# Gathered rows transposed half by DMA, half by TensorE, in the expert loop of a fused attention and mixture-of-experts kernel

## The chip, the cores and the metric

The kernel runs on one core of a Trainium2 chip. A core has five engines with instruction streams of their own: TensorE (PE; its weight loads are shown apart as PEld), VectorE (DVE), ScalarE (ACT), GpSimd (POOL) and SyncE (SP), which here does nothing but issue DMAs. Sixteen DMA engines move data between DRAM and the on-chip memory SBUF; matmuls write to the accumulator memory PSUM. Each engine takes its instructions strictly in order and waits on semaphores.

The metric is the device time in microseconds (us) of one execution, the median of several runs. The kernel before took 1259.69 us (three runs, 1258.86 to 1262.91).

## The reference, cut to what matters

The input is x with 8 sequences of 512 tokens, 512 numbers each, all in 32-bit floats.

```python
xn = layernorm(x)
s = attention(xn)            # 16 heads of 32, linear attention with decay, gate, group norm, Wo
g = silu(ffn(xn))
out = x + s * g

def ffn(xn):                 # over all 4096 tokens
    probs = softmax(xn @ gate_w.T)               # 16 experts
    weights, chosen = top_k(probs, 4); weights /= weights.sum()
    mixed = sum over e of comb[:, e] * ((silu(xn @ Wg[e]) * (xn @ Wu[e])) @ Wd[e])
    shared = (silu(xn @ sWg) * (xn @ sWu)) @ sWd
    return mixed + shared * sigmoid(xn @ shared_gate_w)
```

Each expert is a 512 to 128 to 512 network. Only the four chosen experts of a token count, so the kernel computes only these.

## The kernel before, in words

**Stage one, about 0 to 320 us: routing, and attention of the first two sequences.** Sequences pass through `norm` (statistics on DVE, a power on POOL, centring on DVE; the normalised rows go to the DRAM table `xn_d`), `turn` (transposes on PE, copies on ACT), `route_1`, `route_2` (expert choice) and `share_1`, `share_2` (the shared expert; its result goes to DRAM as `sh_d`). The generator `first` (L882) hands out these pieces, and they are issued between the matmuls of attention for sequence 0. At most three sequences' x are in SBUF at a time (tag `x`, three buffers); `load_x(b + 3)` is issued at the beginning of step b of `first`. `sort` and `table` then put every (token, expert) pair into blocks of 128 rows that belong to one expert: at most 143 blocks (NB). `slot` lists, for each block, which rows of `xn_d` it takes. A row of `xn_d` has 512 floats and 16 expert weights.

**Stage two, about 320 to 795 us: the block loop.** For each block i:

- `gather(i)` (L958): POOL issues an indirect DMA that brings the block's 128 rows from `xn_d` into a buffer `xg` (five of these).
- `transpose_x(i)` (L965): PE loads the offset of the block's expert into a register and transposes the four 128x128 parts of the rows into PSUM; ACT copies the result to `xt` in SBUF.
- `gate_up(i)` (L980): four matmuls of 256 columns (each shown as two records); Silu on ACT and a product on DVE give `slb`.
- `transpose_h(i)` (L993): PE transposes `slb`, DVE copies it to `hT`.
- `down(i)` (L1000): a matmul of 512 columns (two records); DVE scales by the token's expert weight, which stands in the row `xg`, and SP stores `y` to DRAM.

The loop's body (L1023 to L1035) orders these as gate_up(i), transpose_x(i + 2), gather(i + 3), down(i - 1), transpose_h(i). A scheduler then fixes the order on each engine; on PE it is gate_up(i), transpose_x(i + 2), down(i - 1), transpose_h(i). The expert weights of all 16 experts (`wexp`) stay in SBUF during the loop.

**Stage three, about 795 to 1275 us.** Attention of sequences 2 to 7, while `mixture` gathers each token's four rows of `y` and adds them up on POOL and DVE; the output is x + s * silu(...).

Of the kernel before, what the change touches and what calls it, by code (L numbers as in the profile page):

```python
# [10 lines left out]
F32 = mybir.dt.float32  # L11
F16 = mybir.dt.float16
I32 = mybir.dt.int32
U32 = mybir.dt.uint32
AF = mybir.ActivationFunctionType
ALU = mybir.AluOpType
AX = mybir.AxisListType

P = 128
# [4 lines left out]
NC = N // C  # L24
# [69 lines left out]
def tile_block(ctx: ExitStack, tc: tile.TileContext, a: dict, out: bass.AP):  # L94
# [9 lines left out]
        return pp.tile([P, 512], F32, tag=tag, name=name, bufs={"a": 4, "k": 1, "m": 1, "d": 2}[tag])  # L104


    xn_d = dram.tile([B * N, D + E], F32, name="xn_d", tag="xn_d")
    xT_d = [dram.tile([P, KC * N], F32, name=f"xT_d{b}", tag=f"xT_d{b}") for b in range(B)]
    sh_d = [dram.tile([N, D], F32, name=f"sh_d{b}", tag=f"sh_d{b}") for b in range(B)]
    s_d = [dram.tile([N, D], F32, name=f"s_d{b}", tag=f"s_d{b}") for b in range(FIRST)]  # L110
# [112 lines left out]
    def norm(b):  # L223
        xs = xs_of[b]
        mv = p1.tile([P, NC, 2], F32, tag="mv", name=f"mv_{b}", bufs=2)
        rstd = p1.tile([P, NC], F32, tag="rstd", name=f"rstd_{b}", bufs=2)
        tiles = [slice(t, t + 1) for t in range(NC)] if b == 0 else [slice(0, NC)]

        def stand(engine):
            return behind(engine) if b < 2 else nullcontext()  # L230

        def center(ts):
            for t in range(ts.start, ts.stop):
                with stand(DVE):
                    nc.vector.tensor_scalar(
                        xs[:, t, :], xs[:, t, :], mv[:, t, 0:1], rstd[:, t : t + 1],
                        ALU.subtract, ALU.mult)

        for i, ts in enumerate(tiles):
            for t in range(ts.start, ts.stop):  # L240
                st = p1.tile([P, 6], F32, tag="st", name=f"st_{b}_{t}", bufs=4)
                with stand(DVE):
                    nc.vector.bn_stats(st, xs[:, t, :])
                with stand(DVE):
                    nc.vector.bn_aggr(mv[:, t, :], st)
            with stand(POOL):
                nc.gpsimd.tensor_scalar(rstd[:, ts], mv[:, ts, 1], LN_EPS, None, ALU.add)
            with stand(POOL):
                nc.gpsimd.tensor_tensor(
                    rstd[:, ts], rstd[:, ts],  # L250
                    root.to_broadcast([P, ts.stop - ts.start]), ALU.pow)
            if i:
                center(tiles[i - 1])
        center(tiles[-1])
        nc.sync.dma_start(
            xn_d[b * N : (b + 1) * N, :D].rearrange("(t p) d -> p t d", p=P), xs)

    def turn(b):

        xs = xs_of.pop(b)  # L260
        if b:
            xT = p1.tile([P, KC, N], F32, tag="xT1", name=f"xT1_{b}", bufs=2)
        else:
# [81 lines left out]
    def share_2(b):  # L345
        h, sg = h1_of.pop(b), sg_of.pop(b)
        xT1_of.pop(b)
        sh = p1.tile([P, NC, D], F32, tag="sh1", name=f"sh1_{b}", bufs=2)
        for t in range(NC):
            py = bank("dmaa"[t], f"pys_{b}_{t}")  # L350
            with on_pe():
                nc.tensor.matmul(
                    py, lhsT=h[:, t * P : (t + 1) * P], rhs=sw[:, KC * 2 * F :],
                    start=True, stop=True)
            if t % 2:
                nc.vector.tensor_scalar(sh[:, t, :], py, sg[:, t : t + 1], None, ALU.mult)  # L356
            else:
                nc.scalar.activation(sh[:, t, :], py, AF.Copy, scale=sg[:, t : t + 1])
        nc.sync.dma_start(sh_d[b].rearrange("(t p) d -> p t d", p=P), sh)


    def sort():
# [3 lines left out]
        for r in range(TOPK):  # L366
# [2 lines left out]
                w4[:, :, r : r + 1].to_broadcast([P, NT, E]), ALU.mult)  # L369
            if r:  # L370
                nc.gpsimd.tensor_tensor(wt, wt, wr, ALU.add)
        nc.sync.dma_start(xn_d[:, D:].rearrange("(t p) e -> p t e", p=P), wt)
        mf = mask.rearrange("p e t -> p (e t)")
        total = p1.tile([P, E * NT], F32, tag="lT", name="total", bufs=1)
        at = p1.tile([P, E, NT], F32, tag="at", name="at")
# [506 lines left out]
    def first():  # L882

        for b in range(B):
            if b + 3 < B:
                load_x(b + 3)
            route_1(b)
            yield
            share_1(b)
            yield  # L890
            if b + 2 < B:
                norm(b + 2)
            if b + 1 < B:
                turn(b + 1)
                yield
            route_2(b)
            yield
            share_2(b)
            yield
        next(sorting)  # L900
# [48 lines left out]
    for e in range(E - LATE, E):  # L949
        nc.sync.dma_start(wexp[:, e, :], a["experts"][:, e, :])  # L950
    left.close()


    blkp = left.enter_context(
        tc.tile_pool(name="blkp", bufs=1, side="left", reuse_waits="tile"))
    xg_of, xt_of, off_of, h_of, hT_of, done, gone = {}, {}, {}, {}, {}, [], []

    def gather(i):  # L958
        xg = blkp.tile([P, D + E], F32, tag="xg", name=f"xg_{i}", bufs=5)
        nc.gpsimd.indirect_dma_start(  # L960
            out=xg, out_offset=None, in_=xn_d,
            in_offset=bass.IndirectOffsetOnAxis(ap=slot[:, i : i + 1], axis=0))
        xg_of[i] = xg

    def transpose_x(i):  # L965
        with tc.issue_after(done[-1]) if done else nullcontext():
            _, (off_of[i],) = nc.values_load_multi_w_load_instructions(
                of_block(0, i), engines=[mybir.EngineType.PE], min_val=0,
                max_val=(E - 1) * WE, bass_reorder=False,
                skip_runtime_bounds_check_because="sort() takes the minimum with the last place")  # L970
        xg = xg_of[i]
        pt = bank("a", f"pt_{i}")
        for k in range(KC):
            nc.tensor.transpose(  # L974
                pt[:, k * P : (k + 1) * P], xg[:, k * P : (k + 1) * P], ident)
        xt = att.tile([P, KC, P], F32, tag="qT" if i % 2 else "kT", name=f"xt_{i}", bufs=2)
        nc.scalar.copy(xt.rearrange("p k t -> p (k t)"), pt)  # L977
        xt_of[i] = xt

    def gate_up(i):  # L980
        off = off_of[i]
        xt = xt_of.pop(i)
        pg = bank("k" if i % 2 else "m", f"pgu_{i}")
        for k in range(KC):
            nc.tensor.matmul(  # L985
                pg[:, : 2 * F], lhsT=xt[:, k, :], rhs=wflat[:, bass.ds(off + k * 2 * F, 2 * F)],
                start=(k == 0), stop=(k == KC - 1))
        sl = blkp.tile([P, F], F32, tag="sl", name=f"slb_{i}")
        nc.scalar.activation(sl, pg[:, :F], AF.Silu)  # L989
        nc.vector.tensor_tensor(sl, sl, pg[:, F : 2 * F], ALU.mult)  # L990
        h_of[i] = sl

    def transpose_h(i):  # L993
        ph = bank("a", f"ph_{i}")
        done.append(nc.tensor.transpose(ph[:, :P], h_of.pop(i), ident).ins)
        hT = blkp.tile([F, P], F32, tag="hT", name=f"hT_{i}")
        nc.vector.tensor_copy(hT, ph[:, :P])  # L997
        hT_of[i] = hT

    def down(i):  # L1000
        py = bank("d", f"py_{i}")
        nc.tensor.matmul(  # L1002
            py, lhsT=hT_of.pop(i), rhs=wflat[:, bass.ds(off_of.pop(i) + KC * 2 * F, D)],
            start=True, stop=True)
        with tc.issue_after(gone[-1]) if gone else nullcontext():
# [3 lines left out]
                skip_runtime_bounds_check_because="sort() takes the minimum with the last place")  # L1009
        y = att.tile([P, D], F32, tag="tmp", name=f"y_{i}", bufs=TMP)  # L1010
        gone.append(nc.vector.tensor_scalar(  # L1011
            y, py, xg_of.pop(i)[:, bass.ds(at, 1)], None, ALU.mult).ins)
        nc.sync.dma_start(y_d[i * P : (i + 1) * P, :], y)


    for i in range(3):
        gather(i)
    for t in range(NC):
        spill(FIRST - 1, t, project(FIRST - 1, t))
        if t in (1, 2):  # L1020
            transpose_x(t - 1)
    on_of.pop(FIRST - 1)
    for i in range(NB + 1):  # L1023
        if i < NB:
            gate_up(i)
        if i == 2:
            gate_3(FIRST)
        if i + 2 < NB:
            transpose_x(i + 2)
        if i + 3 < NB:  # L1030
            gather(i + 3)
        if i:
            down(i - 1)
        if i < NB:
            transpose_h(i)  # L1035
    left.close()
    right.close()

# [150 lines left out]
```

## Time and profile before

| | before |
|---|---|
| median of the runs | 1259.69 us |
| the profiled execution | 1276.38 us |
| its span, first to last instruction | 1274.6 us |
| mean granted TensorE clock | 0.992 |
| block loop: first gate/up matmul to last down product | 335 to 795 us |
| gathers in the loop (POOL, xg from xn_d) | 143, mean 947 ns of issue |
| stores of y (SP) | 143, 256 KB each |
| DMA traffic | 201 MB, mean 158 GB/s |

How to read it: the page shows one execution, with the profiler on. It was 16.7 us longer than the runs' median. A group's "idle before" is the time in which that engine did nothing just ahead of these instructions, and the name after the arrow is what ended it. An engine that is idle but is not the last to be ready costs nothing. A matmul's record is longer than the spacing of matmuls, because they overlap; spacing is read from start to start.

### The profile page before, as it was taken

The page shows a single profiled execution, that of the slowest core. Times are in us where ns is not written, and L with a number is a line of the kernel's source. Part 1 is how long each engine was busy: PE and PEld are TensorE (multiplying, and loading weights), DVE is VectorE, ACT ScalarE, POOL GpSimd, SP SyncE. Part 2 cuts the span into 40 slices and gives each one's busy share as a digit, 9 for nine tenths or more (in the row PEclk, how much of TensorE's full clock was granted, in tenths as well). Part 3 has the DMA queues.
Part 4 walks back from the last instruction along what each step waited for, and adds up shares of the span by engine and source line. Part 5 has one row for each costly group of instructions (what it writes and reads, how often), then busy time and mean ns, then how long its engine had stood idle before and what let it go on. Part 6 is the DMA issues. An engine that isn't in the chain of part 4 may idle for free. (4 is left out here: it accounts for less than half of the span.)

```text
span 1274.6 us, 21687 instructions
## 1 busy us (share of the span) xinstructions
PE 1218.6 (96%) x8085; PEld 724.0 (57%) x8085; DVE 763.7 (60%) x1668; ACT 343.0 (27%) x623; POOL 423.5 (33%) x398
## 2 busy tenths in 40 slices
PE   7999999989999999999999999999999999989997
PEld 3445544455577777777777776454544544445453
DVE  6377646996233333333333333777969779498784
ACT  3334433121322222222222222114141131311420
POOL 2000003000233222222332321660885857758311
PEclk9999999999999999999999999999999999999999
DMA  9775221450555555555555554840754636435111
GB/s 324 272 278 198 91 109 42 160 204 25 185 168 172 173 168 168 169 166 162 169 174 161 168 168 137 311 141 1 241 172 136 222 98 214 135 121 162 42 33 68
DMA packets 84934, 201.02 MB, mean 158 GB/s; under 512 B 15008, under 2 KB 15776, under 8 KB 82912
## 3 DMA queue, kind: packets, MB, share of 16 engines
q1 hardware_dynamic: 63152, 127.41, 27.5%
q0 software_dynamic: 21680, 72.23, 19.4%
q8 instruction: 67, 1.10, 0.3%
q14 instruction: 35, 0.29, 0.1%
HBM read 127.25 MB, written 72.35 MB: 157 GB/s over the span
## 5 line engine op out<-in xcount | busy, mean ns | idle before, releaser
L960 POOL DMA_INDIRECT xg<-xn_d,slot x143 | 135.4, 947 | 435.1 <-DVE hT L997 323.2
L985 PE MATMUL pgu<-wexp,xt 128*128 x1144 | 270.8, 379 | 0.0
L985 PEld LDWEIGHTS pgu<-wexp,xt 128*128 128x128 f32 x1144 | 206.2, 190 | 63.2 <-ACT xt L977 38.4
L1011 DVE TENSOR_SCALAR y<-py,xg 128x512 f32<-128x512 f32 x143 | 107.4, 751 | 111.4 <-PE py L1002 111.4
L1058 POOL DMA_INDIRECT yg<-y_d,posi x128 | 138.8, 1084 | 47.4 <-DMA m<-sh_d 20.0
L990 DVE TENSOR_TENSOR slb<-slb,pgu 128x128 f32<-128x128 f32 x143 | 41.1, 288 | 185.0 <-ACT slb L989 185.0
L1002 PE MATMUL py<-wexp,hT 128*128 x286 | 146.4, 594 | 0.0
L538 PE MATMUL pv<-wv,xT 128*128 128x512 f32 x256 | 121.0, 611 | 2.9 <-DVE sh L356 1.6
L580 PE MATMUL pk<-xT,wk 128*128 128x512 f32 x256 | 122.2, 618 | 0.0
L989 ACT ACTIVATE slb<-pgu 128x128 f32<-128x128 f32 x143 | 39.6, 277 | 289.1 <-PE pgu L985 289.0
L580 PE MATMUL pq<-xT,wq 128*128 128x512 f32 x256 | 115.9, 593 | 0.0
L709 PE MATMUL pw<-wo,on 128*128 128x512 f32 x224 | 102.6, 603 | 4.9 <-DVE m L1086 4.9
L1093 POOL TENSOR_TENSOR xo<-xo,m 128x512 f32<-128x512 f32 x30 | 44.7, 1492 | 168.2 <-DVE m L1086 162.5
L977 ACT COPY xt<-pt 128x512 f32<-128x512 f32 x143 | 83.8, 586 | 39.1 <-PE pt L974 39.1
L974 PE MATMUL pt<-ident,xg 128*128 128x128 f32 x572 | 86.5, 274 | 5.8 <-DMA xg<-xn_d,slot 4.2
L974 PEld LDWEIGHTS pt<-ident,xg 128*128 128x128 f32 x572 | 69.4, 141 | 27.4 <-PE pgu L985 10.1
L650 DVE TENSOR_TENSOR sc<-ps,dmask 128x512 f32<-128x512 f32 x128 | 79.4, 682 | 1.4 <-PE ps L634 1.4
L538 PEld LDWEIGHTS pv<-wv,xT 128*128 128x128 f32 x256 | 46.4, 193 | 59.5 <-issue 54.0
L580 PEld LDWEIGHTS pq<-xT,wq 128*128 128x128 f32 x256 | 47.3, 191 | 52.2 <-issue 51.4
L580 PEld LDWEIGHTS pk<-xT,wk 128*128 128x128 f32 x256 | 47.0, 194 | 49.0 <-issue 46.7
L709 PEld LDWEIGHTS pw<-wo,on 128*128 128x128 f32 x224 | 41.8, 193 | 55.0 <-issue 46.5
L585 ACT ACTIVATE sk<-pk 128x512 f32<-128x512 f32 x32 | 19.0, 595 | 128.5 <-PE pk L580 110.1
(160 smaller groups left out, 1577.3 us busy)
## 6 DMA issues: line engine op xcount, KB each, us to landing
y_d<-y SPq DMA_DIRECT2D x143, 256.0 KB
wexp<-in_experts SPq DMA_DIRECT2D x16, 768.0 KB
xn_d<-x SPq DMA_DIRECT2D x8, 1024.0 KB
sh_d<-sh SPq DMA_DIRECT2D x8, 1024.0 KB
m<-sh_d SPq DMA_DIRECT2D x32, 256.0 KB
xo<-in_x SPq DMA_DIRECT2D x32, 256.0 KB
out<-xo SPq DMA_DIRECT2D x32, 256.0 KB
x<-in_x SPq DMA_DIRECT2D x7, 1024.0 KB
```

Of the source, the lines that this page charges most:

```text
L538: nc.tensor.matmul(pv, lhsT=xT_of[b][:, k, t * P : (t + 1) * P], rhs=wv[:, k, :], start=(k == 0), stop=(k == KC - 1))
L580: nc.tensor.matmul(ps, lhsT=w[:, k, g * P : (g + 1) * P], rhs=xT_of[b][:, k, :], start=(k == 0), stop=(k == KC - 1))
L650: nc.vector.tensor_tensor(s, pss[j].rearrange("p (c t) -> p c t", t=C), dmask[:, g * HG + j].unsqueeze(1).to_broadcast([P, NC, C]), ALU.mult)
L709: nc.tensor.matmul(pw, lhsT=on_of[b][:, g, t * P : (t + 1) * P], rhs=wo[:, g, :], start=(g == 0), stop=(g == G - 1))
L960: nc.gpsimd.indirect_dma_start(out=xg, out_offset=None, in_=xn_d, in_offset=bass.IndirectOffsetOnAxis(ap=slot[:, i : i + 1], axis=0))
L974: nc.tensor.transpose(pt[:, k * P : (k + 1) * P], xg[:, k * P : (k + 1) * P], ident)
L977: nc.scalar.copy(xt.rearrange("p k t -> p (k t)"), pt)
L985: nc.tensor.matmul(pg[:, : 2 * F], lhsT=xt[:, k, :], rhs=wflat[:, bass.ds(off + k * 2 * F, 2 * F)], start=(k == 0), stop=(k == KC - 1))
L1002: nc.tensor.matmul(py, lhsT=hT_of.pop(i), rhs=wflat[:, bass.ds(off_of.pop(i) + KC * 2 * F, D)], start=True, stop=True)
L1011: gone.append(nc.vector.tensor_scalar(y, py, xg_of.pop(i)[:, bass.ds(at, 1)], None, ALU.mult).ins)
L1058: nc.gpsimd.indirect_dma_start(out=yg, out_offset=None, in_=y_d, in_offset=bass.IndirectOffsetOnAxis(ap=posi[:, r, g : g + 1], axis=0))
L1093: nc.gpsimd.tensor_tensor(xo, xo, m, ALU.add)
```

## The change

What it does, part by part:

- **The table.** `xn_d` is now declared as 16-bit integers, with the same bytes per row. The first 256 floats of a row are stored as before. The last 256 floats are stored as two runs of 256 16-bit values: all lower halves, then all upper halves. The new function `halves(b)` makes them: for each of a sequence's four tiles, a POOL copy sorts the halves into `hs` (four buffers) and SP stores `hs`. It stands in `first` after `norm(b + 2)`; `load_x(b + 3)` moves from the head of the step to behind it.
- **Memory.** `share_2` uses six buffers of one tile each, not two of four tiles, and stores each tile by itself: four DMAs of 256 KB in place of one of 1 MB. For the loop there are seven row buffers (`homes`), three of them in one of the buffers of `v`; the row buffers are fixed tiles used in turn.
- **The transpose.** For block i SP issues one DMA transpose (`turn_rows`) of the 512 16-bit values of the second half, 128 rows, into one of four places in `pls`. PE transposes only the first two of the four parts. `join(i)` on ACT copies these two from PSUM, and writes the transposed lower and upper halves in turn into the other half of `xt`, so that each pair is a float again. `xt` has two buffers where it had four.
- **The stagger.** The body is now turn_rows(i + 2), join(i + 1), gate_up(i), transpose_x(i + 2), transpose_h(i - 1), down(i - 2), gather(i + 4), and runs for one step more. `sl` and `hT` get two buffers. The register load of the expert's offset moves from `transpose_x` to the head of `gate_up`.

```diff
-    xn_d = dram.tile([B * N, D + E], F32, name="xn_d", tag="xn_d")
+    xn_d = dram.tile([B * N, 2 * (D + E)], U16, name="xn_d", tag="xn_d")
...
         nc.sync.dma_start(
-            xn_d[b * N : (b + 1) * N, :D].rearrange("(t p) d -> p t d", p=P), xs)
+            xn_d[b * N : (b + 1) * N, :D].rearrange("(t p) d -> p t d", p=P),
+            xs[:, :, : D // 2].bitcast(U16))
+
+    def halves(b):
+        xs = xs_of[b]
+        for t in range(NC):
+            hs = p1.tile([P, D], U16, tag="hs", name=f"hs_{b}_{t}", bufs=4)
+            with behind(POOL):
+                nc.gpsimd.tensor_copy(
+                    hs.rearrange("p (h d) -> p h d", h=2),
+                    xs[:, t, D // 2 :].bitcast(U16).rearrange("p (d h) -> p h d", h=2))
+            g = b * NC + t
+            nc.sync.dma_start(xn_d[g * P : (g + 1) * P, D : 2 * D], hs)
+        xs_of.pop(b)
...
-        sh = p1.tile([P, NC, D], F32, tag="sh1", name=f"sh1_{b}", bufs=2)
         for t in range(NC):
+            sh = p1.tile([P, D], F32, tag="sh1", name=f"sh1_{b}_{t}", bufs=6)
...
-        nc.sync.dma_start(sh_d[b].rearrange("(t p) d -> p t d", p=P), sh)
+            nc.sync.dma_start(sh_d[b][t * P : (t + 1) * P, :], sh)
...
         for b in range(B):
-            if b + 3 < B:
-                load_x(b + 3)
             route_1(b)
             yield
             share_1(b)
             yield
             if b + 2 < B:
                 norm(b + 2)
+            halves(b)
+            if b + 3 < B:
+                load_x(b + 3)
...
+    more = att.tile([P, 2 * NC * D], U16, tag="v", name="more", bufs=2)
+    homes = [blkp.tile([P, ROW], U16, tag=f"xg{j}", name=f"xg{j}") for j in range(4)]
+    homes += [more[:, j * ROW : (j + 1) * ROW] for j in range(3)]
+    pls = [att.tile([P, 2, KC, P], U16, tag="kT", name=f"pl{j}", bufs=2) for j in range(2)]
...
+    def turned(i):
+        return pls[i % 2][:, i // 2 % 2]
+
+    def turn_rows(i):
+        if i < NB:
+            nc.sync.dma_start_transpose(turned(i), row(i)[:, D : 2 * D])
+
     def transpose_x(i):
+        if i < NB:
+            pt_of[i] = bank("a", f"pt_{i}")
+            for k in range(KP):
+                nc.tensor.transpose(
+                    pt_of[i][:, k * P : (k + 1) * P],
+                    row(i).bitcast(F32)[:, k * P : (k + 1) * P], ident)
+
+    def join(i):
+        if i < NB:
+            xt = att.tile([P, KC, P], F32, tag="qT", name=f"xt_{i}", bufs=2)
+            nc.scalar.copy(
+                xt[:, :KP, :].rearrange("p k t -> p (k t)"), pt_of.pop(i)[:, : KP * P])
+            nc.scalar.copy(
+                xt[:, KP:, :].bitcast(U16).rearrange("p k (t h) -> p h k t", h=2),
+                turned(i).rearrange("p (h k) t -> p h k t", h=2))
+            xt_of[i] = xt
...
-    for i in range(NB + 1):
-        if i < NB:
-            gate_up(i)
+    join(0)
+    for i in range(NB + 2):
+        turn_rows(i + 2)
+        join(i + 1)
+        gate_up(i)
         if i == 2:
             gate_3(FIRST)
-        if i + 2 < NB:
-            transpose_x(i + 2)
-        if i + 3 < NB:
-            gather(i + 3)
-        if i:
-            down(i - 1)
-        if i < NB:
-            transpose_h(i)
+        transpose_x(i + 2)
+        transpose_h(i - 1)
+        down(i - 2)
+        gather(i + 4)
```

In the scheduled order of the changed kernel, SP takes the transpose of block k + 7 directly behind the store of y of block k, and the store of y of block k + 1 behind that transpose. On ACT the join of the DMA's halves stands ahead of the copy from PSUM, and both ahead of Silu of the block before.

## The prediction

> **What bounds the kernel now.** I began with the summary at the head of the page, which names the busiest engine:
>
> ```profile
> PE 1218.6 (96%) x8085; PEld 724.0 (57%) x8085; DVE 763.7 (60%) x1668; ACT 343.0 (27%) x623; POOL 423.5 (33%) x398
> ```
>
> TensorE (PE) is busy for 96% of the span, but its ends are modelled, so I went to the stage that the change is about. The windows view gives the block loop (410 to 780 us) and then two single blocks, one from the middle and one from the loop's end:
>
> ```profile
> 410.00:780.00 370.00, 365.90 (x1736) 270.33 (x1735) 142.57 (x347) 99.92 (x232) 109.60 (x116) 1.00 0.53 168
> 503.37:506.51 3.14, 3.14 (x17) 2.36 (x16) 1.24 (x3) 0.87 (x3) 0.94 (x1) 1.00 0.52 170
> 788.76:791.53 2.77, 2.77 (x13) 1.91 (x11) 1.23 (x3) 0.28 (x1) 0.00 (x0) 1.00 0.28 104
> ```
>
> The columns are length, then PE, PE weight loads, VectorE (DVE), ScalarE (ACT), GpSimd (POOL), clock, DMA share, GB/s. 116 blocks in 370 us are 3.19 us each; an undisturbed one takes 3.14 us. The third row is a block with nothing left to transpose (13 matmuls, not 17): 2.77 us. Four transposes are therefore worth 0.36 us or a little more. The timeline, PE alone, splits a block by start times:
>
> ```profile
> 503.37 1.02 PE L1002 MATMUL py<-wexp,hT 128*128 x2
> 504.24 0.27 PE L995 MATMUL ph<-ident,slb 128*128 128x128 f32 x1
> 504.34 1.89 PE L985 MATMUL pgu<-wexp,xt 128*128 x8
> 506.07 0.60 PE L974 MATMUL pt<-ident,xg 128*128 128x128 f32 x4
> 506.51 1.02 PE L1002 MATMUL py<-wexp,hT 128*128 x2
> ```
>
> From start to start: down 0.87, transpose of h 0.10, gate/up 1.73, four transposes of x 0.44 (0.43 in the block before). Nothing is idle between them, so in this stage PE alone sets the time, and a transpose costs 0.107 us, not the 0.274 us of its record. Everything else has room: per block ACT 0.87, DVE 1.24, POOL 0.94 us, and the DMA engines 0.53 x 3.19 = 1.7 us. The groups say how often PE waited there:
>
> ```profile
> L974 PE MATMUL pt<-ident,xg 128*128 128x128 f32 x464 | 70.1, 274 | 4.1 <-DMA xg<-xn_d,slot 3.8
> L977 ACT COPY xt<-pt 128x512 f32<-128x512 f32 x116 | 67.9, 585 | 33.4 <-PE pt L974 33.4
> L989 ACT ACTIVATE slb<-pgu 128x128 f32<-128x128 f32 x116 | 32.1, 277 | 237.7 <-PE pgu L985 237.7
> ```
>
> 3.8 us in 370 are late gathers. One is visible: POOL issued a gather at 495.63 and its transpose began only at 499.77, after an idle 0.23; so 4.1 us from issue to use, while another with 3.84 us (492.40 to 496.24) made it.
>
> [...] the multiplication by cos (L589) takes 676 ns in 100:200, where POOL does nothing, and 1032 and 1180 ns (qT, kT) in 1000:1100, where POOL adds tiles.
>
> **Part 1, two of four transposes leave PE.** 143 x 2 x 0.107 = 30.7 us, as long as PE stays the bound at 3.14 - 0.21 = 2.92 us a block.
>
> **Part 2, the DMA transpose (143, 128 KB each, on SP's queue).** Unknown, so bounded. [...] A gain below nothing is excluded: the queues had no such work. I estimate [...] with issue, start and completion like a gather's, 3 us from issue to landing. Three tests then:
> - *DMA engines*: [...] They become the bound above 1.2 us per transpose, and the gain is gone at about 1.4.
> - *SP*: a store of y issues in 0.33 us (timeline). In the order after, SP alternates: transpose of block k+7, store of y of block k+1. It waits at the transpose for the gather, and that store stands behind it; y has four buffers, so a microsecond there hurts nobody. SP needs 0.33 + the transpose's issue, under 2.92 unless issue alone exceeds 2.5 us.
> - *The loop through the buffers*: seven row buffers, so gather k+7 waits for y of k. From there: y 0.75, to POOL 0.27, gather 4.0 to landing, transpose T, join 1.0, handover 0.1; then three block periods from gate/up to y. Seven periods in all, hence 4 periods = 6.1 + T. At 2.92 us a period T may be 5.5 us, at 3.14 us 6.4. My 3 us leaves 2.5.
>
> **Part 3, the joining on ACT.** The copy from PSUM halves: between 277 ns (128 wide) and 585 ns (512), so 0.38. The join is 512 elements: 0.6, at worst 1.2 if its two-byte strided writes run at half rate. With Silu 1.3 to 1.9 of 2.92: hidden. The join waits for the DMA and Silu of the block before queues behind it; Silu's result is wanted one block later than before (the deeper stagger), and that is the cover. If the DMA is more than about 2.5 us late, gate/up itself is late next.
>
> **Part 4, the stagger.** The transposition of h and the down projection now come one and two blocks after gate/up: no PE time, one more drain step at the end, about 0.5 us. PE's register load of the expert offset moves from two blocks ahead to directly before the first gate/up matmul. What covers it is the queued down work, 0.87 us, where before it was gate/up matmuls of 0.21 each; I take 0 and keep 0.3 us a block as the bad end. Row buffers 5 to 7: the gather gets nearly 7 us from issue to the PE transpose instead of 4; half of the late gathers, 2 us, is gained. The first transposes at entry: +0.5.
>
> **Part 5, the first stage pays for the halves.** 32 POOL copies of 128x512 16-bit elements. [...] the two-input adds here take 1.28 us. [...] DVE's two-input rotations there are some 25 us of work, a fifth of the time beside POOL: about +1 us. The stores to DRAM carry the same bytes in 24 (shared expert) + 32 (halves) more issues, about 0.35 us each, which stand in SP's queue. What counts is the loads of x, now behind them:
>
> ```profile
> 63.40 1.31 SPq L145 DMA_DIRECT2D x<-in_x  x1
> 75.26 0.36 SPq L255 DMA_DIRECT2D xn_d<-x  x1
> 78.56 1.28 DVE L243 BATCH_NORM_STATS2 st<-x 128x6 f32<-128x512 f32 x2
> 80.00:90.00 10.00, 10.00 (x30) 3.99 (x29) 8.53 (x20) 1.62 (x3) 1.26 (x2) 1.00 0.74 258
> 100.00:110.00 10.00, 9.52 (x69) 4.39 (x69) 8.96 (x37) 5.94 (x8) 0.00 (x0) 1.00 0.89 319
> ```
>
> The fifth sequence's x (counting from 0) was loaded at 63.40, for statistics at 78.56. After the change SP holds that load behind the store of sequence 4, which stood at 75.26: it starts at about 77 and, at 1 MB, lands near 83. DVE, in order, stands for 4 to 5 us. It is 85 to 90% busy here, PE is the bound, so most of it is absorbed by work already in PE's queue until about 108, where PE already waits for DVE. I take 3.5 us of PE time [...] range 0 to 12.
>
> **Sum.** -30.7 - 2 + 4.5 + 1.0 (entry and drain) + 1.2 (a block in ten whose join is late by about 0.1, as with gathers today) = -26. The profiled execution took 1276.4 us (span 1274.6), so 1250 by it; the runs' median is 16.7 us lower, and nothing suggests that the difference lies in these steps: 1259.7 - 26 = **1234 us**.
>
> **Rivals.**
> - *The DMA transpose bounds the loop (ends slower).* Place: the 16 engines, or the transposes one after another. It decides from 1.4 us of engine time, or 2.8 us in series with the store's issue. At 2.0 us of engine time a block takes 3.7 us: +0.5 x 143 = +70, about 1330 us[...]. For it: two-byte elements scattered over partitions, on queues already 53% busy. [...] 24%.
> - *The wait returns through the buffers.* T between 5.5 and 6.7 us: each further us is 36 us, so 1246 to 1275. For it: gathers are already late now and then at 4 us. 10%.
> - *PE's sequencer or the first stage eats it.* A register load exposed by 0.3 us is 43 us, with the sum above 1277; or 12 us of first-stage stalls, 1242. 6%.
> - *Better than said*, below 1222, if the first stage absorbs all and the gathers' waits all go: 3%. That the change doesn't do what it says is excluded: the order shows two transposes per block on PE instead of four.
>
> The forecast keeps 57%, with a range of its own of 1222 to 1246. About 0.3% (4 us) is what a measurement of this kernel can tell. The second rival's 10% fall 4 faster, 2 within, 4 slower, the third's 6% half within and half slower. Faster: 57 + 3 + 4 = 64%; within 0.3%: 2 + 3 = 5%; slower: 24 + 4 + 3 = 31%. For 8 in 10 the range must reach into the first rival to its milder half: 1222 to 1335.
>
> **What would show it.** Right: blocks of 2.9 us in the middle of the loop; PE without idle before gate/up; ACT about 1.3 us a block; the weight loads of gate/up not waiting for the join. Wrong: gate/up waiting for ACT and ACT for the DMA of the transposed halves; a DMA share near 1; SP's transposes with long issues; in the first stage, DVE waiting at the statistics around 80 us for x, and PE idle near 108 us for DVE.

## The result, and the profile after

The changed kernel took 1250.41 us (median of seven runs, 1248.2 to 1256.08); the kernel before, beside it, 1260.88 us (seven runs). The ratio is 0.9916, with a 95% interval of 0.9895 to 0.9937: faster by 10.5 us, where 26 were forecast. The profiled execution took 1250.12 us, its span is 1248.4 us.

The head of the page after, with TensorE's granted clock in 40 slices of the span:

```profile
PE 1188.4 (95%) x7799; PEld 703.8 (56%) x7799; DVE 772.1 (62%) x1668; ACT 399.7 (32%) x766; POOL 448.9 (36%) x430
...
PEclk9979899999989999999999999999989999999999
```

PE lost 30 us of work (1218.6 before), ACT gained 57, POOL 25. The third, fifth and twelfth digit of the clock, slices around 78, 140 and 359 us, are below 9; in the page before all forty are 9:

```profile
PEclk9999999999999999999999999999999999999999
```

That is the first hint of where the gain went.

The loop did what was said. The windows view of the kernel after, the loop's middle and one block (columns as in the prediction):

```profile
400.00:760.00 360.00, 359.41 (x1599) 267.48 (x1598) 151.54 (x369) 154.30 (x369) 115.69 (x123) 1.00 0.94 227
500.80:503.71 2.91, 2.91 (x14) 2.19 (x13) 1.24 (x3) 1.27 (x3) 0.94 (x1) 1.00 0.97 188
```

123 blocks in 360 us: 2.93 us each, PE idle for 0.6 us in all. But the DMA share rose from 0.53 to 0.94. The timeline of PE for that block:

```profile
500.80 1.89 PE L1030 MATMUL pgu<-wexp,xt 128*128 x8
502.53 0.38 PE L1004 MATMUL pt<-ident,xg 128*128 128x128 f32 x2
502.74 0.27 PE L1042 MATMUL ph<-ident,slb 128*128 128x128 f32 x1
502.85 1.02 PE L1051 MATMUL py<-wexp,hT 128*128 x2
503.71 0.38 PE L1030 MATMUL pgu<-wexp,xt 128*128 x1
```

From start to start: gate/up 1.73, two transposes 0.21, transpose of h 0.11, down 0.86: 2.91 us, for the 2.92 of the prediction. The groups on ACT:

```profile
L1013 ACT COPY xt<-pl 128x512 uint16<-128x512 uint16 x143 | 109.6, 767 | 156.3 <-DMA pl<-xg 92.3 <-DMA pl<-more 63.8
L1011 ACT COPY xt<-pt 128x256 f32<-128x256 f32 x143 | 51.3, 359 | 0.0
```

The join takes 0.77 us and waits for the DMA transpose in 135 of 143 blocks, 156 us in all; PE hardly sees it, with 0.7 us of idle before gate/up in the whole loop.

The gain was lost ahead of the loop. The first gate/up matmul starts at 357.6 us, 22.6 us later than before (335.0). One place shows how; the timelines of SP, of DVE and of PE in the kernel after, in this order:

```profile
62.64 1.18 SPq L270 DMA_DIRECT2D xn_d<-hs  x2
63.92 0.40 SPq L147 DMA_DIRECT2D x<-in_x  x1
```

```profile
71.16 0.69 DVE L245 BATCH_NORM_STATS2 st<-x 128x6 f32<-128x512 f32 x1 [3.42 <-DMA x<-in_x]
71.77 0.67 DVE L572 COPY g<-pg 128x512 f32<-128x512 f32 x1
```

```profile
72.54 2.04 PE L577 MATMUL pf<-g,four 128*128 128x512 f32 x2 [4.61 <-issue]
```

The same in the kernel before:

```profile
41.25 0.58 SPq L145 DMA_DIRECT2D x<-in_x  x1
```

```profile
67.68 0.69 DVE L555 COPY g<-pg 128x512 f32<-128x512 f32 x1 [0.27 <-PE pg L551]
68.29 1.28 DVE L243 BATCH_NORM_STATS2 st<-x 128x6 f32<-128x512 f32 x2
```

```profile
68.47 1.10 PE L560 MATMUL pf<-g,four 128*128 128x512 f32 x2 [0.86 <-issue]
```

The load of x of sequence 4 leaves SP at 63.92 us (41.25 before), behind stores of the halves. Its statistics on DVE wait 3.42 us for it. Behind them on DVE stands the copy `g`, which PE needs (the matmuls of `pg` ahead of it end at 67.9 us, it begins at 71.77), and PE stands for 4.61 us. So two things came together: x is late, and the scheduled order on DVE has the statistics ahead of `g`, where before `g` stood ahead of them. Then comes what the prediction did not have at all. The windows view of the kernel after; look at the clock, third column from the end:

```profile
66.00:70.00 4.00, 1.94 (x11) 0.27 (x9) 0.69 (x1) 0.00 (x0) 0.00 (x0) 1.00 0.88 250
70.00:74.00 4.00, 1.46 (x2) 0.50 (x2) 2.54 (x5) 0.00 (x0) 0.00 (x0) 0.50 1.02 413
78.00:82.00 4.00, 3.87 (x19) 3.88 (x19) 2.79 (x4) 3.35 (x8) 2.52 (x4) 0.50 0.31 101
86.00:90.00 4.00, 4.00 (x10) 1.61 (x9) 1.43 (x7) 1.54 (x3) 0.00 (x0) 0.87 1.03 370
```

PE's last work before the gap ends at 67.9 us. From 70.0 to about 87 us the clock is at half (0.50), and the two matmuls of `pf` take 2.04 us where they took 1.10 before. The clock falls 2.1 us after the last work, and comes back 14.5 us after work begins again, 9 us after the last of two small gaps (0.78 and 0.67 us). A gap of 2.7 us before 121.5 us was followed by 10 us at 0.50, one of 2.8 us at the loop's entry by 3.4 us of it. But a gap of 3.06 us before 30.74 us in the same trace was followed by work at 1.00; what decides it is not shown. Behind the three gaps of 4.61, 2.73 and 2.83 us, work of 6.5, 4.6 and 1.7 us was lost at the lower clock (PE's busy time times what the clock lacks of 1). Where PE sets the time, these three then cost 1.6 to 2.7 times their length, an estimate from these numbers.

### The profile page after: what moved, and what is told of

The parts are those of the page before. It is cut to its first block, busy times and chain, and to the rows that moved or that the text cites. A ratio compares the mean times of both kernels' runs of the same rounds, so it can differ in the third digit from the quotient of the medians.

```text
span 1248.4 us, 21569 instructions
## 1 busy us (share of the span) xinstructions
PE 1188.4 (95%) x7799; PEld 703.8 (56%) x7799; DVE 772.1 (62%) x1668; ACT 399.7 (32%) x766; POOL 448.9 (36%) x430
## 3 DMA queue, kind: packets, MB, share of 16 engines
q8 instruction: 64, 1.05, 0.3%
## 5 line engine op out<-in xcount | busy, mean ns | idle before, releaser
L1030 PEld LDWEIGHTS pgu<-wexp,xt 128*128 128x128 f32 x1144 | 217.4, 191 | 92.6 <-issue 32.1
L989 POOL DMA_INDIRECT xg<-xn_d,slot x83 | 78.4, 945 | 287.6 <-DVE y L1060 172.0
L1013 ACT COPY xt<-pl 128x512 uint16<-128x512 uint16 x143 | 109.6, 767 | 156.3 <-DMA pl<-xg 92.3
L1107 POOL DMA_INDIRECT yg<-y_d,posi x128 | 141.9, 1108 | 49.5 <-DMA m<-sh_d 22.1
L989 POOL DMA_INDIRECT more<-xn_d,slot x60 | 56.4, 941 | 114.4 <-DVE y L1060 113.5
L1060 DVE TENSOR_SCALAR y<-py,xg 128x512 f32<-128x512 f32 x83 | 62.3, 750 | 31.4 <-PE py L1051 31.4
L1060 DVE TENSOR_SCALAR y<-py,more 128x512 f32<-128x512 f32 x60 | 45.0, 750 | 20.7 <-PE py L1051 20.6
```

The lines of the kernel that those rows point to most:

```text
L989: nc.gpsimd.indirect_dma_start(out=row(i), out_offset=None, in_=xn_d, in_offset=bass.IndirectOffsetOnAxis(ap=slot[:, i : i + 1], axis=0))
L1013: nc.scalar.copy(xt[:, KP:, :].bitcast(U16).rearrange("p k (t h) -> p h k t", h=2), turned(i).rearrange("p (h k) t -> p h k t", h=2))
L1030: nc.tensor.matmul(pg[:, : 2 * F], lhsT=xt[:, k, :], rhs=wflat[:, bass.ds(off + k * 2 * F, 2 * F)], start=(k == 0), stop=(k == KC - 1))
L1060: gone.append(nc.vector.tensor_scalar(y, py, row(i).bitcast(F32)[:, bass.ds(at, 1)], None, ALU.mult).ins)
L1107: nc.gpsimd.indirect_dma_start(out=yg, out_offset=None, in_=y_d, in_offset=bass.IndirectOffsetOnAxis(ap=posi[:, r, g : g + 1], axis=0))
```

## The experiments

The kernel before did not take the same time in all sets of runs: 1261 to 1264 us in some, 1273 to 1274 in others. So each set is read by its ratio to the kernel before in the same set, and traces by stages. Four moments, in us from the start of each trace: the slot table written on DVE (end of the first stage), first gate/up matmul, last down matmul, span.

| run | slot table | first gate/up | last down | span | median | before, median | ratio [95%] |
|---|---|---|---|---|---|---|---|
| before, first profile | 317.7 | 335.0 | 794.7 | 1274.6 | 1260.88 | | |
| after, first profile | 335.9 | 357.6 | 781.9 | 1248.4 | 1250.41 | 1260.88 | 0.9916 [0.9895, 0.9937] |
| e0_before | 314.4 | 331.7 | 793.6 | 1271.7 | 1273.49 (one run) | 1273.11 | |
| e1_early_halves | 323.7 | 341.9 | 764.2 | 1242.3 | 1244.72 | 1273.11 | 0.9788 [0.9769, 0.9808] |
| e2_join_behind | 335.8 | 353.6 | 778.5 | 1257.5 | 1258.71 | 1273.11 | 0.9887 [0.9869, 0.9905] |
| e3_both | 325.2 | 343.0 | 765.8 | 1244.7 | 1248.90 | 1273.11 | 0.9820 [0.9801, 0.9838] |
| e4_after | 335.7 | 354.9 | 778.6 | 1244.6 | 1246.51 | 1263.43 | 0.9876 [0.9857, 0.9895] |
| e5_halves_on_act | 327.3 | 346.3 | 768.8 | 1236.0 | 1235.28 | 1263.43 | 0.9777 [0.9757, 0.9797] |
| e6_stagger_only | 316.4 | 333.8 | 784.0 | 1249.4 | 1250.01 | 1263.43 | 0.9898 [0.9882, 0.9915] |
| e7_twice | 336.6 | 355.6 | 850.8 | 1316.8 | 1318.59 | 1263.43 | 1.0435 [1.0415, 1.0455] |
| e8_stores_by_pool | 324.6 | 343.4 | 768.1 | 1238.2 | 1245.27 | 1262.69 | 0.9860 [0.9831, 0.9889] |
| e10_one_store_pool | 342.0 | 361.3 | 788.0 | 1257.5 | 1255.42 | 1262.69 | 0.9942 [0.9925, 0.9960] |
| e11_no_copies | 323.5 | 342.8 | 766.6 | 1243.8 | 1245.90 | 1273.88 | 0.9781 [0.9749, 0.9814] |
| e12_sort_in_loop | 314.8 | 332.6 | 776.5 | 1254.8 | 1256.61 | 1273.88 | 0.9882 [0.9851, 0.9912] |
| e13_pool_all | 334.5 | 353.5 | 781.5 | 1248.7 | 1250.61 | 1262.66 | 0.9907 [0.9884, 0.9930] |
| e14_pool_one_store | 328.7 | 347.6 | 774.2 | 1243.7 | 1246.23 | 1262.66 | 0.9874 [0.9850, 0.9897] |
| e15_stats_behind | 322.2 | 341.3 | 763.0 | 1235.6 | 1239.26 | 1274.07 | 0.9743 [0.9711, 0.9775] |
| e16_stats_act | 321.5 | 340.5 | 764.9 | 1238.2 | 1240.56 | 1274.07 | 0.9753 [0.9726, 0.9780] |

### The 16 us of the first profile

> The kernel before, unchanged, profiled once more; the question is where its first profiled execution (1276.4 us) got the 16 us that its runs' median (about 1260) doesn't have. Theory A, one odd execution: a span near 1259 us, first gate/up matmul again at 335 us; the 16 us are then missing from the block loop (first gate/up to last y near 445 instead of 460 us) or from what follows it (near 470 instead of 479 us), and the gain of the change in the loop is smaller than the first two traces say. Theory B, the profiled execution of this kernel is always longer than its other runs: a span near 1275 us again, loop 460 us, rest 479 us.

The span was 1271.7 us, but so were the other runs of that set: 1273.11 us is their median, profiled or not. Neither theory holds as written. From last down to the end the traces of this set take 478 to 479 us, as the first profile of before does (479.9); the first profile of after and the set of e4_after take 465 to 467 us, whichever kernel runs. So the 16 us lie mostly behind the loop and don't belong to the change. In the first profile PE there waited 8.9 us for its own issue before matmuls of `pk`, `ps` and `po`, and not at all in the first profile of after. What sets that was not tried.

### The order in the first stage, and the entry

The changed kernel again, beside others on one chip:

> The changed kernel unchanged, as the measure for the other runs of this set on one chip. From the stages of the runs so far (first stage to the slot table +21 us against the kernel before on the same chip, entry +4, block loop -37, rest 0): 12 us under the kernel before, 1258 to 1263 us where that one takes 1273, loop 424 us. If instead the loop's gain depends on the chip: a loop outside 420 to 428 us.

Loop 423.7 us, as expected; the time is 16.9 us under the kernel before, where 12 were expected and the first comparison gave 10.5; the two intervals just meet.

e1_early_halves:

```diff
         for b in range(B):
+            if b + 3 < B:
+                load_x(b + 3)
...
                 norm(b + 2)
-            halves(b)
-            if b + 3 < B:
-                load_x(b + 3)
             if b + 1 < B:
+                halves(b + 1)
                 turn(b + 1)
```

> The changed kernel with its first stage in another order: the sorting of sequence b+1's halves follows norm(b+2), one step earlier than needed, and the load of x of sequence b+3 stands at the head of the step as in the kernel before. Same work, same DMAs. Theory 1, late loads of x (they stand behind the halves, and those on POOL behind the statistics of a later sequence) let PE run dry, and an idle of some 3 us is followed by half the granted clock: the first gate/up matmul comes at 340 to 345 us instead of 357.5, DVE waits for x at the statistics about 4 us instead of 12.9, no half clock between 60 and 140 us, time 1232 to 1238 us. Theory 2, the POOL copies [...] and the 56 more DMA issues are what costs: first gate/up still near 357 us, time 1248 to 1252 us.

The ratio falls to 0.9788. The first gate/up at 341.9 us and DVE's wait of 5.1 us for x are about what theory 1 said, and PE's stop before `pf` is 0.81 us again, with the clock at 1.00 behind it. The edit moves the loads, and with them the scheduled order on DVE: `g` stands ahead of the statistics again. So it doesn't part the two. Not all comes back: the slot table is still 9.3 us later than in e0_before, half the clock is not gone, and 1244.72 us lies above the 1232 to 1238 of theory 1, in a set in which the kernel before took 1273. The timelines of e1_early_halves, DVE and then PE, show where:

```profile
107.71 1.29 DVE L245 BATCH_NORM_STATS2 st<-x 128x6 f32<-128x512 f32 x2 [1.61 <-DMA x<-in_x]
...
110.72 0.75 DVE L370 TENSOR_SCALAR sh<-pys,sg 128x512 f32<-128x512 f32 x1
...
111.98 0.75 DVE L370 TENSOR_SCALAR sh<-pys,sg 128x512 f32<-128x512 f32 x1
```

```profile
112.79 2.67 PE L650 MATMUL ps<-qT,kT 32*128 32x128 f32 x20 [4.08 <-DVE sh L370]
```

PE stands 4.08 us for `sh`, and half the clock follows until about 119 us. In the kernel before the two `sh` come first and the statistics of the last sequence after them.

e2_join_behind holds the first join behind the attention copies on ACT; e3_both is e1_early_halves and this.

```diff
-            nc.scalar.copy(xt[:, :KP, :]..., pt_of.pop(i)...)
-            nc.scalar.copy(xt[:, KP:, :]..., turned(i)...)
+            with behind(ACT) if i == 0 else nullcontext():
+                nc.scalar.copy(xt[:, :KP, :]..., pt_of.pop(i)...)
+            with behind(ACT) if i == 0 else nullcontext():
+                nc.scalar.copy(xt[:, KP:, :]..., turned(i)...)
```

> The changed kernel with one edit at the entry of the block loop: the first block's two joining copies are held behind the four attention copies on ACT, instead of the join standing ahead of three of them. Theory 1, the join of block 0 waits 8 us for the first DMA transpose and holds the attention copies, PE idles 2.8 us and then runs at half clock for 4 us: the entry is 4 us shorter, time about 1246 us. Theory 2, PE would wait at the first gate/up for that same transpose anyway: gate/up waits about as long, time 1249 to 1251 us.

> Both edits, of the first stage's order and of the entry. Theory 1: the gains add, first gate/up matmul at 336 to 341 us, time 1228 to 1234 us, faster than both kernels. Theory 2: near 1250 us, the first stage's cost is in the copies and issues, the entry's in the transposes' latency.

The timelines of ACT and of PE of the kernel after, where this edit bites:

```profile
350.90 0.76 ACT L1013 COPY xt<-pl 128x512 uint16<-128x512 uint16 x1 [8.04 <-DMA pl<-xg]
351.54 1.05 ACT L896 COPY so<-pw 128x512 f32<-128x512 f32 x2
```

```profile
352.16 5.40 PE L726 MATMUL pw<-wo,on 128*128 128x512 f32 x8 [2.83 <-ACT so L896]
```

In e2's trace the entry (slot table to first gate/up) is 17.8 us instead of 21.7, so theory 1 holds there. In the time it can't be told apart: the ratio 0.9887 lies between the two of the changed kernel, whose entry took 19.2 us in e4_after. e3_both is no better than e1_early_halves, whose entry is 18.2 us without the edit: the gains don't add, and its theory 1 fails.

### The copies: on POOL, on ACT, none

e5_halves_on_act is e1_early_halves with `nc.scalar.copy` for `nc.gpsimd.tensor_copy`; e11_no_copies stores four constant tiles in place of the sorted ones.

> As e1_early_halves, with the sorting copies of the halves on ACT instead of POOL. Theory 1, what is left of the first stage's cost is the contention between POOL's copies and DVE (four centrings take 3.06 us beside POOL's copies and 1.92 us without): centrings back to 1.92 us, the PE idle of 4.1 us near 112 us and the half clock after it gone, first gate/up matmul at 333 to 337 us instead of 341.9, time 6 to 9 us under e1_early_halves. Theory 2, the 56 more DMA issues in SP's queue delay what stands behind them: as e1_early_halves, within 2 us. Theory 3, ACT's copies then come late for PE: slower than e1_early_halves by 3 to 10 us.

> As e1_early_halves, but the 32 copies that sort the halves are left out: the same 32 stores bring a constant to the table, so what the block loop computes is not the reference's. Of the 9 us that the first stage still lost in e1_early_halves (slot table at 323.7 against 314.4 us), theory 1 puts it on the copies, which slow DVE's centrings beside them from 480 to 765 ns each: slot table at 315 to 318 us, no PE idle over 1.5 us near 112 us, time 5 to 8 us under e1_early_halves by the ratio (0.972 to 0.975). Theory 2, the stores themselves, their issues and their traffic on queues that are full in the first 45 us: slot table still at 322 to 325 us, ratio 0.978 to 0.980.

With POOL's copies a centring takes 0.82 us (median in e1_early_halves), without them 0.54 (e5_halves_on_act and e11_no_copies). Through what the copies slow it is not shown. The prediction had looked only at DVE's two-input rotations; a centring has one tile as input. Yet the time doesn't care: ratios 0.9777 and 0.9781 beside 0.9788, slot table of e11_no_copies at 323.5 us, and the same stop, 3.45 us for `sh` at 111 us. The 32 copies cost DVE 6.4 us (32 times 0.743 - 0.542), all of it covered by other waits. Theory 1 of both falls.

### SP's queue

```diff
-            nc.sync.dma_start(xn_d[g * P : (g + 1) * P, D : 2 * D], hs)
+            nc.gpsimd.dma_start(xn_d[g * P : (g + 1) * P, D : 2 * D], hs)
```

That is e13_pool_all, over e1_early_halves; e14_pool_one_store also stores `sh` once per sequence, with two `hs` buffers. e8_stores_by_pool and e10_one_store_pool are the same two with the copies on ACT.

> As e5_halves_on_act, with the 32 stores of the sorted halves issued by POOL instead of SP. What is left of the first stage's cost there is about 10 us. Theory 1, it is SP's queue: the loads of x stand behind the additional stores. Then first gate/up at 336 to 341 us instead of 346.3, and a ratio to the kernel before of 0.971 to 0.974 (e5_halves_on_act: 0.9777). Theory 2, it is the copies' work on ACT, late for DVE and PE: no change, ratio 0.976 to 0.979. Theory 3, POOL's issues hold up DVE: slower, above 0.980.

> As e8_stores_by_pool, and the shared expert's result again in one store of 1 MB for each sequence from two large buffers, as in the kernel before, so that SP has 24 issues less; to make room the sorted halves have two buffers instead of four. Theory 1 (SP's queue): first gate/up at 334 to 338 us, ratio 0.969 to 0.972. Theory 2 (ACT's work): as e5_halves_on_act, 0.976 to 0.979, or above it, since ACT then waits for the stores of the halves.

> As e1_early_halves, with the 32 stores of the sorted halves issued by POOL, directly behind its own copies, instead of SP. Theory 1, SP's queue is what is left: slot table at 316 to 320 us (e1_early_halves: 323.7, kernel before on that chip: 314.4), time 4 to 7 us under e1_early_halves, ratio 0.973 to 0.976. Theory 2, the order on DVE (statistics of sequence 6 ahead of the shared expert's products that PE waits for) and the traffic: slot table at 322 to 326 us, ratio 0.978 to 0.981.

> As e13_pool_all, and the shared expert's result again in one store of 1 MB a sequence; the sorted halves have two buffers instead of four, and only POOL waits for them. SP then issues in the first stage what it does in the kernel before. Theory 1 (SP's queue): slot table at 314 to 317 us, ratio 0.971 to 0.974. Theory 2 (traffic and DVE's order): 322 to 326 us, 0.978 to 0.981.

None gained; all four are above e1_early_halves. With the copies on ACT, PE stood for ACT (1.75 and 1.71 us in e8, 5.92 us in e10, where ACT waited 28.8 us in all for `hs` buffers). With all on POOL single centrings took up to 1.2 us and PE stood 3.6 us at 32 us and 4.4 us at 76 us in e13. So fewer issues on SP were no help in these forms. Each brought a wait of its own on another engine, so the queue's share in what is left is not excluded by them.

### The order on DVE

e15_stats_behind; e16_stats_act has the copies on ACT besides.

```diff
-                with stand(DVE):
+                with tc.issue_after(of_sh[b - 4]) if b > 6 else stand(DVE):
                     nc.vector.bn_stats(st, xs[:, t, :])
...
-                nc.vector.tensor_scalar(sh, py, sg[:, t : t + 1], None, ALU.mult)
+                of_sh[b] = nc.vector.tensor_scalar(
+                    sh, py, sg[:, t : t + 1], None, ALU.mult).ins
```

> As e1_early_halves, with one more constraint: the statistics of sequence 7 on DVE may not be put ahead of the products of the shared expert of sequence 3, as in the kernel before. Theory 1, this order is what is left of the first stage's cost (PE stands 4.1 us, and half the clock for 5 us follows): slot table 7 to 9 us earlier against the kernel before on the same chip (1 to 3 us late instead of 9.3), ratio 0.972 to 0.975. Theory 2, the additional traffic delays DVE's inputs wherever they stand: PE stands elsewhere for as long, ratio 0.978 to 0.981.

> As e15_stats_behind, with the sorting copies on ACT as in e5_halves_on_act. Theory 1: centrings at 0.54 us instead of 0.8 give DVE another few us of room, ratio 0.970 to 0.974. Theory 2: ACT's own queue then holds up PE, ratio as e15_stats_behind or 0.002 to 0.005 above it.

The timeline of PE in e15_stats_behind, the same matmul:

```profile
113.44 1.15 PE L651 MATMUL ps<-qT,kT 32*128 32x128 f32 x14 [0.27 <-DVE lT L301]
```

The 4.08 us have become 0.27: the stop went with the order on DVE. The ratio is 0.9743, as theory 1 said, 34.8 us under the kernel before and the lowest here; but its interval meets that of e1_early_halves, and the slot table, at 322.2 us, is only 1.5 us earlier than there, where 7 to 9 were expected. Of the 6.7 us between the spans of the two traces 5.5 lie behind the loop, where the edit does nothing. So a gain of the edit in whole time is not shown. In this execution PE ran at half clock from 70 to 80 us, around three gaps of 0.6 to 0.8 us:

```profile
70.00:72.00 2.00, 1.61 (x8) 0.04 (x3) 0.76 (x2) 0.45 (x1) 1.92 (x4) 0.50 1.03 346
76.00:78.00 2.00, 2.00 (x8) 1.72 (x9) 0.53 (x5) 0.78 (x3) 0.00 (x0) 0.50 1.10 367
```

The kernel before and e1_early_halves had such gaps too (0.6 to 0.9 us, near 70 us) and no half clock behind them. The six executions of e15 spread from 1233.3 us (mean clock 0.995) to 1247.9 (0.985). e16 doesn't differ from e15. PE's idle from 20 us to the slot table is almost that of e0_before again (16.0 and 15.1 us); of the 7.8 us that e15 is still later there, about 5 are lost to the clock.

### The loop: stagger alone, and two DMA transposes

e6_stagger_only has before's first stage and table; from the change it takes the seven buffers, the order of the body and the place of the register load.

```diff
-    KP = KC // 2
+    KP = KC
...
-            nc.sync.dma_start_transpose(turned(i), row(i)[:, D : 2 * D])
...
-            nc.scalar.copy(xt[:, KP:, :]..., turned(i)...)
```

> The kernel before with its first stage, and the changed kernel's stagger, seven row buffers and place of the register load, but all four transposes on PE and none by DMA. Theory 1, the loop's gain is that of the two transposes: block 3.14 to 3.18 us, loop 449 to 455 us (before: 461.9), time 6 to 12 us under the kernel before for the late gathers and the waits that it had. Theory 2, deeper stagger and buffers give most of the gain: loop under 440 us. Theory 3, the register load in its new place costs: loop above 462 us.

Windows of the same stretch, first e0_before, then e6_stagger_only, then e4_after:

```profile
400.00:740.00 340.00, 335.24 (x1595) 248.61 (x1594) 131.16 (x319) 91.72 (x213) 100.14 (x106) 1.00 0.53 167
```

```profile
400.00:740.00 340.00, 340.00 (x1628) 260.42 (x1627) 138.73 (x325) 93.48 (x217) 102.36 (x109) 1.00 0.54 171
```

```profile
400.00:740.00 340.00, 338.02 (x1502) 251.29 (x1501) 142.30 (x347) 145.28 (x347) 108.63 (x115) 1.00 0.92 227
```

The last count of POOL is the gathers, one a block: 3.20, 3.12 and 2.95 us. PE's idle of 1.4% is gone with the stagger alone. From first gate/up to last down the loop takes 461.9 us in e0_before, 450.2 here, 423.7 in e4_after: 11.7 us by stagger and buffers (9.5 against the 459.7 of the first profile of before), 26.5 by the transposes. And in whole time, e6_stagger_only with none of the sorting and none of the DMA transposes is only 3.5 us slower than the full change, and their intervals overlap.

e7_twice adds one line after the transpose of each block, `nc.sync.dma_start_transpose(spare[i % 2], row(i)[:, :D])`.

> The changed kernel with a second DMA transpose for each block, of the first half of the row, into a spare buffer that nothing reads; PE still transposes its two parts. Theory 1, a transpose takes about 1.05 us of all 16 DMA engines (2.75 us a block with one), so these become the bound: 3.8 us a block, loop 540 to 550 us, time 1370 to 1390 us, SP waiting for transposes and long issues. Theory 2, the engines' share overstates what is taken and SP's issue is the bound (2 x 1.25 + 0.52 = 3.0 us): loop 430 to 445 us. Theory 3, neither: loop 424 us as with one.

It lies between theories 1 and 2: the loop takes 495.2 us, 3.46 a block. The timeline of SP:

```profile
504.19 0.53 SPq L1065 DMA_DIRECT2D y_d<-y  x1
504.81 1.23 SPq L1000 DMA_TRANSPOSE pl<-more  x1
506.13 1.24 SPq L1001 DMA_TRANSPOSE spare<-more  x1
507.47 0.54 SPq L1065 DMA_DIRECT2D y_d<-y  x1
```

SP issues one behind the other, with 0.1 us between: 3.28 us from store to store, where theory 2 had counted 3.0 without the gaps. A transpose's issue is hardly longer than with one a block (1.20). In this stretch SP is the bound; why the loop's average is higher still was not followed. The DMA share is 1.09 in 500 to 600 us, so it isn't an occupancy that ends at 1, and the 0.94 of one transpose was not yet a wall.

### Sorting in the loop

e12_sort_in_loop keeps the table of plain floats and sorts after the gather:

```diff
+            with behind(POOL):
+                nc.gpsimd.tensor_copy(
+                    hss[i % 2].rearrange("p (h d) -> p h d", h=2),
+                    row(i)[:, D // 2 : D].bitcast(U16).rearrange("p (d h) -> p h d", h=2))
-            nc.sync.dma_start_transpose(turned(i), row(i)[:, D : 2 * D])
+            nc.sync.dma_start_transpose(turned(i), hss[i % 2])
```

> The sorting of the halves moved out of the first stage altogether: the table holds plain floats as in the kernel before, and in the loop POOL sorts the second half of each gathered row into one of two buffers, from which the DMA transpose takes it. Gathers run one block further ahead. Theory 1, the first stage alone ate the gain: first gate/up at 334 to 338 us as without sorting, loop 424 us as in the changed kernel (POOL 0.95 + 0.8 us of 2.93 a block, about 1 us more in the loop through the buffers, where 2 us are free), time 1224 to 1232 us where the kernel before takes 1263 (ratio 0.969 to 0.976). Theory 2, the longer way makes the transposes late: the join waits, PE with it, loop 440 us or more, ratio above 0.98. Theory 3, POOL's copies beside DVE's work on the blocks slow DVE: loop 424 to 435 us.

The first stage is as good as before (slot table 314.8 us, first gate/up 332.6), but the loop takes 443.9 us. Its group of gate/up matmuls between 400 and 740 us:

```profile
L1020 PE MATMUL pgu<-wexp,xt 128*128 x887 | 211.6, 381 | 12.4 <-ACT xt L1000 12.3
```

PE waits 12.4 us for the join there (2.0 in e4_after): theory 2. The added step makes the join late; through which buffer it does so was not followed. The time is no better than that of the changed kernel. Beside e11_no_copies (slot table 323.5 us), which has the stores and not the copies, it shows that what is left of the first stage's cost comes with the added stores and the order around them, not with the copies.

## Why the prediction was wrong

The direction and the loop were right, the sum was not. By its steps:

- **Part 1, two transposes, -30.7 us.** The undisturbed block is 2.91 us (2.92 said). Alone, against e6_stagger_only, they brought 26.5 us. Of the rest 2 us are late joins (PE's wait for `xt` in e4_after); what is left was not followed.
- **Part 2, the DMA transpose.** The trace of before has none; that its engine time would stay under the bound of 1.2 us, and so the case against the first rival, was not shown. It is about 1.05 us, an estimate from the kernel after and e6_stagger_only (0.94 x 2.93 less 0.54 x 3.12): near that bound, but hidden. Issue is 1.2 us, so SP is busy for 1.9 of 2.93 us with its gaps; from issue to landing it is 3.6 us in the median, where 3 was estimated after the gather's and 5.5 allowed, and to the join's start 3.8 and 4.4 us in two blocks near 500 us. The first rival (+70 us and more) did not come about, because its unknown stayed under its threshold, though not by much; with a second transpose SP's issue was met first (e7_twice).
- **Part 3.** 0.77 us for the join (0.6 said, up to twice that by the author's estimate), 1.27 us of ACT a block: hidden.
- **Part 4.** The register load cost nothing: e6_stagger_only has it in the new place and the shortest block with four transposes (3.12 us, 3.20 in e0_before). The 0.3 us of the bad end was the author's estimate. The gain was undersized: 2 us were booked for late gathers, 9.5 to 11.7 came. The profile before showed it in part, 3.19 us on average against 3.14 undisturbed, which is 7 us over 143 blocks, but only the waits put down to DMA were counted. Where the rest came from was not followed.
- **Part 4, entry, +0.5 us.** 1.9 to 4.4 us, because the join of block 0 stands ahead of attention's copies on ACT; with it behind them 0.5 is left (e2_join_behind, 17.8 us for 17.3 before).
- **Part 5, the first stage, +4.5 us (3.5 for the late load, 1 for DVE beside POOL), range 0 to 12.** This is the step that failed: 18 to 19 us (335.9 against 317.7; e4_after against e6_stagger_only, 335.7 against 316.4). Its kind was right: statistics on DVE that wait for x, and PE behind them. Three terms of it were wrong. It followed one load, of sequence 5; the longest stop came from sequence 4, whose load moved by 22.7 us, and DVE's waits for x went from 4.4 us in all to 12.9, since each load now stands behind the store of the sequence before, which waits for that sequence's statistics. It took the order on DVE as it was, and the statistics moved ahead of `g`. And it priced a gap on PE at its length, where half the clock (0.50) followed three of them; that term it had put at nothing. The windows view in slices of 1 us, from 20 us to the slot table, sizes the last: PE's idle grows from 14.8 us before to 23.7 after, and the time lost to the clock (PE's busy time times what the clock lacks of 1) from 3.4 to 14.3. That is 8.9 + 10.9 us where 18.2 were lost, so more than half is clock. e1, with the loads in their old place and the order on DVE that comes with it, brings the ratio from 0.988-0.992 to 0.979. e15 removes one more stop, by the order on DVE alone; what that is worth in whole time is not shown. The copies took POOL 0.75 us each on average in the kernel after. DVE beside POOL, booked at 1 us, lost 6.4 us on its centrings, and the kernel nothing measurable (ratios 0.9788 with the copies, 0.9781 without).
- **The shift by 16.7 us** from profile to median was right in the main: 13.4 of those us lie behind the loop, if the first profile of after is the measure.

In all, by stages: first stage +18 to +21, entry +2 to +4, loop -35 to -38, rest 0: together -13 us between the first two profiles and -15 between e0_before and e4_after, where the two comparisons gave -10.5 and -16.9. The loop as a whole came a little better than its forecast of -31, and that is partly luck: 26.5 us for 30.7 and about 10 for 2. The rival "PE's sequencer or the first stage eats it", at 6%, was nearest: its first stage of 12 us gave 1242.

## What to carry to other kernels

When a loop is bought with work in another stage, cost that stage as closely as the loop: for each load that moves, follow who stands in order behind its first reader, and ask for every later round, not for one. Three gaps of 2.7 to 4.6 us on TensorE cost by estimate 1.6 to 2.7 times their length here, so such a gap is not safely priced at its length. Look at the order on an engine anew in the changed kernel: here the scheduled order on DVE moved with the loads. And try the free part of a change alone: here the stagger without any of the new work gave 13.4 of 16.9 us.

## What was not expected of the hardware

- Three gaps of 2.7 to 4.6 us on TensorE in the kernel after were followed by 3.4 to 14.5 us of work at a granted clock of 0.50; one of 3.06 us in the same trace was not. Three gaps of 0.6 to 0.8 us close together came with it in e15_stats_behind, and similar ones in the kernel before did not.
- A DMA transpose of 128 rows of 512 two-byte values, SBUF to SBUF, took 1.2 us to issue on SP and 3.6 us from issue to landing, and came with about 1.05 us more busy time of all 16 engines a block; the store of y beside it went from 0.32 us of issue (the kernel before) to 0.52 and from 2.0 us to landing (e6_stagger_only) to 3.1.
- One-input centrings on DVE took 0.82 us (median) in e1_early_halves with the copies on POOL, and 0.54 us in e11_no_copies without them and in e5_halves_on_act with the copies on ACT.
- The part behind the loop, the same in all kernels, took 465 to 470 us in the sets where the kernel before needed 1261 to 1264 us, and 472 to 480 us in the others. The first profile of the kernel before, an execution of 1276.38 us, goes with the latter.
